# Closing a second scatter table at expert 50 and adding its rows between the last experts of a mixture-of-experts layer

## The chip, the cores and the metric

The kernel runs on one core of a Trainium2 chip. The metric is the device time of one execution in microseconds (us). A core has five engines that run side by side, each through its own queue of instructions: TensorE (PE in the profile; PEld is its weight load), VectorE (DVE), ScalarE (ACT), GpSimd (POOL) and SyncE (SP). SP, ACT and POOL also issue DMA transfers; all of them are carried by the same 16 DMA engines of the core.

## The reference, cut to what matters

The program is a stack of two gated blocks on 2048 tokens of width 512: a token-routed cross-attention layer, a quantized feed-forward layer, a real attention layer and, last, a mixture of experts. The change lies in the mixture of experts alone:

```python
E, K, H, F = (64, 6, 512, 192)
# each token picks K=6 of 64 experts; an expert takes at most CAP=96 slots here
h = silu(einsum('ech,ehf->ecf', buf, w_gate)) * einsum('ech,ehf->ecf', buf, w_up)
out = einsum('ecf,efh->ech', h, w_down)
y = segment_sum(gathered * w, tok, num_segments=Tn)      # each row back to its token
shared = silu(x @ ws_gate) * (x @ ws_up) @ ws_down       # one expert that sees all tokens
return (y + shared)
x = x + tanh(g_ffn[1]) * (y + shared)
```

So the output of a token is its residual row, plus six weighted expert rows, plus the shared expert's row.

## The kernel before, in words

Three stages come first (two layers up to about 520 us, then attention and routing up to about 920 us). Routing leaves in DRAM the normalized rows with their expert weights (`h_rows`), and in SBUF the table `idx`, which says for each expert which token sits in each of its 96 slots. The residual rows have been stored in `out` already (line 897). The shared expert's hidden values of all 16 row tiles lie in SBUF (`shared_a`, 128 rows by 192, for each tile), its down weights too (`shared_dn`).

The expert stage is a loop over 64 experts (line 1195), written as a software pipeline. Iteration `e` issues, in this order of the program:

- `gather(e + 6)`: POOL fetches the 96 rows of a later expert by an indirect DMA (line 1129) into one of six `xg` buffers.
- `turn(e + 2)`: four TensorE transposes of the gathered rows (line 1142), and a DVE copy to `gT` (line 1144).
- `turn_hidden(e)`: two transposes of the hidden values (line 1165), and a DVE copy to `eaT` (line 1167).
- `hidden(e + 1)`: gate and up product in one PSUM tile `gu_ps` (line 1152), Silu on ACT (line 1154), the product with the routing weight on DVE (line 1156).
- `finish(e)`: the down product `e_y` (line 1175), a copy to one of four `e_o` buffers on ACT (line 1177), and an indirect DMA on POOL that adds the 96 rows into a table in DRAM (line 1178). Then the weights of expert `e + 15` are loaded into the buffers that expert `e` leaves (`load_expert`, lines 756, 757 and 759, all issued by SP).

The adding DMAs are kept from overlapping on one table, so the kernel has two tables: even experts add into `out`, odd ones into `more_rows`, which was filled with zeros at the start (line 315). From expert 61 on (`LAST = 3`) all add into `out`. After iteration 61 the program allocates six `rest` tiles in the `e_gu` buffers of experts that are done and loads the 16 row tiles of `more_rows` into them (line 1211, SP). After the loop, for each of the 16 tiles: two transposes of the shared hidden values (`turn_shared`, lines 1217 and 1219), the shared down product `sh_y` (line 1227), one DVE instruction that scales it and adds it to the tile of `rest` (line 1229), and a plain POOL DMA that adds the tile into its 128 rows of `out` (line 1230).

PSUM tiles come from two pools: three buffers for the transposes (`ps_t`) and five for the products (`ps_m`); the shared expert uses the same ones. Weights sit in two pools, `ew` with eight buffers and `ew2` with seven, so 15 experts are loaded ahead. This loop isn't under `manual_schedule`, unlike the stages before it: the framework's planner sets each engine's order from the program order and its own costs, and adds the waits. On DRAM tensors it goes by the regions that an access names: a scatter names the whole table, `out[:, :]`, a plain add 128 rows of it.

Of the kernel before, what the change touches and what calls it, by code (L numbers as in the profile page):

```python
# [9 lines left out]
F32 = mybir.dt.float32  # L10
# [4 lines left out]
ALU = mybir.AluOpType  # L15
# [4 lines left out]
P = 128  # L20
B, S, D = 4, 512, 512
T = B * S
NT = T // P
# [13 lines left out]
E, TOPK, F, GRP = 64, 6, 192, 8  # L37
FH = F // 2
# [8 lines left out]
def flamingo_kernel(  # L47
# [21 lines left out]
    nc = tc.nc  # L69
# [12 lines left out]
    more_rows = dram.tile([TP, D], F32, name="more_rows")  # L82
# [17 lines left out]
    ident = keep.tile([P, P], F32, name="ident")  # L100
# [14 lines left out]
    def after(ins, others):  # L115

        for other in others:
            tc.add_manual_dep(
                ins.ins, other.ins.name, mybir.DependencyInfo(mybir.DependencyClass.Sync, mybir.DependencyReason.DATA),
                reason="what the table holds",  # L120
            )
# [63 lines left out]
    with (  # L185
# [114 lines left out]
        with tc.tile_pool(name="route0", bufs=1) as rp:  # L300
# [54 lines left out]
            while step < NT:  # L355
                a, o = scan[cur], scan[1 - cur]
# [72 lines left out]
        tg_at, half_f1, w_gain, tg_f0_256 = (factors[:, i : i + 1] for i in range(4))  # L429
# [320 lines left out]
    ew = ctx.enter_context(tc.tile_pool(name="ew", bufs=8, side="right"))  # L750
    loaded = {}

    def load_expert(e, ew):

        gu = ew.tile([P, 2, KC, F], F32, name="e_gu", tag="e_gu")
        nc.sync.dma_start(gu[:, 0, :, :], e_gate[e].rearrange("(p k) f -> p k f", k=KC))
        nc.sync.dma_start(gu[:, 1, :, :], e_up[e].rearrange("(p k) f -> p k f", k=KC))
        dn = ew.tile([FH, 2, D], F32, name="e_dn")
        nc.sync.dma_start(dn, e_down[e].rearrange("(p c) d -> p c d", c=2))
        loaded[e] = gu, dn, ew  # L760
# [3 lines left out]
    shared_a = moe.tile([P, NT, F], F32, name="shared_a")  # L764
    shared_dn = moe.tile([FH, 2, D], F32, name="shared_dn")
# [7 lines left out]
    with (  # L773
# [284 lines left out]
        for n in range((NT + 5) * KC):  # L1058
            j, i = divmod(n, KC)
# [39 lines left out]
            else:  # L1099
# [7 lines left out]
                if j == NT:  # L1107
                    at_pool.__exit__(None, None, None)
                    context_pool.__exit__(None, None, None)
                    ew2 = ctx.enter_context(tc.tile_pool(name="ew2", bufs=7))  # L1110
# [3 lines left out]
    with (  # L1114
        tc.tile_pool(name="ex", bufs=2) as xp,
        tc.tile_pool(name="ps_g", bufs=3, space=PSUM) as ps_t,
        tc.tile_pool(name="ps_e", bufs=5, space=PSUM) as ps_m,
    ):

        idx = xp.tile([CAP, E], I32, name="idx", bufs=1)  # L1120
        after(nc.scalar.dma_start(idx, taken[1 : CAP * E + 1, :].rearrange("(s e) o -> s (e o)", e=E)), taken_by)


        tables = out, more_rows
        LAST = 3
        gathered = {}
        def gather(e):
            g = xp.tile([CAP, D + E], F32, name="xg", bufs=6)
            nc.gpsimd.indirect_dma_start(  # L1129
                out=g[:, :],  # L1130
                out_offset=None,
                in_=h_rows[:, :],
                in_offset=bass.IndirectOffsetOnAxis(ap=idx[:, e : e + 1], axis=0),
            )
            gathered[e] = g

        def turn(e):

            g = gathered.pop(e)
            ps = ps_t.tile([P, KC, CAP], F32, name="g_ps", tag="t")  # L1140
            for k in range(KC):
                nc.tensor.transpose(ps[:, k, :], g[:, bass.ts(k, P)], ident[:CAP, :CAP])  # L1142
            gT = xp.tile([P, KC, CAP], F32, name="gT", bufs=3)
            nc.vector.tensor_copy(gT, ps)  # L1144
            return g, gT

        def hidden(e, g, gT):

            gu = loaded[e][0]
            ps = ps_m.tile([CAP, 2, F], F32, name="gu_ps", tag="m")  # L1150
            for k in range(KC):
                nc.tensor.matmul(ps, gT[:, k, :], gu[:, :, k, :], start=k == 0, stop=k == KC - 1)  # L1152
            s = xp.tile([CAP, F], F32, name="s")
            nc.scalar.activation(s, ps[:, 0, :], AF.Silu)  # L1154
            a = xp.tile([CAP, F], F32, name="a")
            nc.vector.scalar_tensor_tensor(  # L1156
                a.rearrange("q (c p) -> q p c", c=2), s.rearrange("q (p c) -> q p c", c=2),
                g[:, D + e : D + e + 1], ps[:, 1, :].rearrange("q (p c) -> q p c", c=2), ALU.mult, ALU.mult,
            )
            return a  # L1160

        def turn_hidden(a):
            ps = ps_t.tile([FH, 2, CAP], F32, name="ea_ps", tag="t")
            for c in range(2):
                nc.tensor.transpose(ps[:, c, :], a[:, bass.ts(c, FH)], ident[:CAP, :CAP])
            aT = xp.tile([FH, 2, CAP], F32, name="eaT")
            nc.vector.tensor_copy(aT, ps)
            return aT

        def finish(e, aT):  # L1170

            _, dn, held = loaded.pop(e)
            y = ps_m.tile([CAP, D], F32, name="e_y", tag="m")
            for c in range(2):
                nc.tensor.matmul(y, aT[:, c, :], dn[:, c, :], start=c == 0, stop=c == 1)  # L1175
            o = xp.tile([CAP, D], F32, name="e_o", bufs=4)
            nc.scalar.copy(o, y)  # L1177
            nc.gpsimd.indirect_dma_start(  # L1178
                out=tables[e % 2 if e < E - LAST else 0][:, :],
                out_offset=bass.IndirectOffsetOnAxis(ap=idx[:, e : e + 1], axis=0),  # L1180
                in_=o[:, :],
                in_offset=None,
                compute_op=ALU.add,
            )
            later = e + ew.bufs + ew2.bufs
            if later < E:
                load_expert(later, held)


        AHEAD = 6  # L1190
        for e in range(AHEAD):
            gather(e)
        turned = {0: turn(0), 1: turn(1)}
        acts = {0: hidden(0, *turned.pop(0))}
        for e in range(E):
            if e + AHEAD < E:
                gather(e + AHEAD)
            if e + 2 < E:
                turned[e + 2] = turn(e + 2)
            aT = turn_hidden(acts.pop(e))  # L1200
            if e + 1 < E:
                acts[e + 1] = hidden(e + 1, *turned.pop(e + 1))
            finish(e, aT)
            if e == E - LAST:


                rest = []
                for held in (ew, ew, ew, ew, ew2, ew2):
                    rest.append(held.tile([P, 3, D], F32, name="rest", tag="e_gu"))
                for j in range(NT):  # L1210
                    nc.sync.dma_start(rest[j // 3][:, j % 3, :], more_rows[bass.ts(j, P), :])


        def turn_shared(j):
            ps = ps_t.tile([FH, 2, P], F32, name="a_ps", tag="t")
            for c in range(2):
                nc.tensor.transpose(ps[:, c, :], shared_a[:, j, bass.ts(c, FH)], ident)
            aT = xp.tile([FH, 2, P], F32, name="aT")
            nc.scalar.copy(aT, ps)
            return aT  # L1220

        aT = turn_shared(0)
        for j in range(NT):
            y = ps_m.tile([P, D], F32, name="sh_y", tag="m")
            this, aT = aT, turn_shared(j + 1) if j + 1 < NT else None
            for c in range(2):
                nc.tensor.matmul(y, this[:, c, :], shared_dn[:, c, :], start=c == 0, stop=c == 1)
            o = rest[j // 3][:, j % 3, :]
            nc.vector.scalar_tensor_tensor(o, y, half_f1, o, ALU.mult, ALU.add)
            nc.gpsimd.dma_start(out[bass.ts(j, P), :], o, accum_op=ALU.add)  # L1230


# [27 lines left out]
```

## Time and profile before

| what | value |
|---|---|
| median of three runs | 1287.63 us (1286.29 to 1292.52) |
| the profiled execution, its own time | 1289.68 us |
| its span in the profile | 1287.9 us |
| TensorE busy | 1036.6 us (80% of the span) |
| VectorE busy | 797.3 us (62%) |
| ScalarE busy | 568.6 us (44%) |
| GpSimd busy | 385.4 us (30%) |
| DMA, by SP's queue | 128.04 MB, 33.2% of 16 engines' span |
| DMA, by POOL's queue | 45.16 MB, 18.0% of 16 engines' span |
| scatters of expert rows, issue to landing | 3.9 / 9.2 / 10.5 us (least, median, most) |
| loads of `rest`, issue to landing | median 6.2 us |
| adds of `rest` into `out`, issue to landing | median 9.7 us |

The span runs from the first to the last instruction of the program on the core; the time of the execution is 1.8 us longer. Shares of busy time are averages over stages with quite different limits, so what the change is worth has to be read from the expert stage, and there from its last 120 us. A transfer's time "to landing" runs from the start of the instruction that issues it to the moment when its semaphore says that all data are there.

### The profile page before, as it was taken

To read this page: it belongs to the slowest core of one execution; us is meant where nothing else is said; L and a number is where in the kernel's file an instruction comes from. 1 tells how busy PE (TensorE), PEld (TensorE's weight loads), DVE (VectorE), ACT (ScalarE), POOL (GpSimd) and SP (SyncE) were. 2 spreads that over 40 slices of the span, in tenths; PEclk is the share of its full clock that TensorE was granted. 3 is DMA by queue.
4 is the path that set the end of the run, shared out by engine and by line. 5 is a ranking of instruction groups with operands and counts; after the bars stand their busy time and mean duration, and the time that the engine had idled before them with its cause. 6 is when DMAs were issued, how large, how long until landed. Compare 5 with 4: busy or idle time off the path is not lost.

```text
span 1287.9 us, 14860 instructions
## 1 busy us (share of the span) xinstructions
PE 1036.6 (80%) x4603; PEld 526.6 (41%) x4603; DVE 797.3 (62%) x1981; ACT 568.6 (44%) x1128; POOL 385.4 (30%) x538
## 2 busy tenths in 40 slices
PE   4498999358888887679888888883499999999994
PEld 3244444123433333344444444441255555544441
DVE  7799999769999997547667676664122222222221
ACT  3766665366767564455555555540011111111120
POOL 3023222100000000012343434346244444444434
PEclk9698999769999999688999999996699999999997
DMA  9844343311111111961111110007699999999978
GB/s 331 293 105 108 91 98 81 83 33 33 33 17 17 21 22 20 279 192 43 60 43 60 43 52 27 36 28 196 179 295 271 279 263 269 271 275 272 265 207 137
DMA packets 75805, 174.75 MB, mean 136 GB/s; under 512 B 13024, under 2 KB 14064, under 8 KB 75664
## 3 DMA queue, kind: packets, MB, share of 16 engines
q1 hardware_dynamic: 51696, 128.04, 33.2%
q0 software_dynamic: 23200, 45.16, 18.0%
q8 instruction: 37, 0.61, 0.2%
q10 hardware_dynamic: 832, 0.62, 0.2%
q14 instruction: 40, 0.33, 0.1%
HBM read 133.76 MB, written 44.20 MB: 138 GB/s over the span
## 4 chain that ended last, share of the span: by engine, by line
DVE 34%; PE 32%; DMA 19%; ACT 7%; issue 5%; POOL 2%; SPq 0%; DVEq 0%; POOLq 0%; ACTq 0%
DMA out_dram<-e_o,idx 13%; PE gu_ps L1152 5%; PE at_s L833 4%; PE at_o L884 4%; PE l_mm L473 3%; DVE mx_top L586 3%; DVE low L838 3%; PE e_y L1175 3%; PE p_ps L857 3%; DVE inter L655 3%; PE first_ps L934 3%; DVE mx_q L602 3%; DVE w_q L265 2%; DVE w_src L262 2%; ACT p L847 2%
## 5 line engine op out<-in xcount | busy, mean ns | idle before, releaser
L1152 PE MATMUL gu_ps<-e_gu,gT 128*96 128x384 f32 x512 | 179.6, 494 | 0.2 <-DVE gT L1144 0.2
L838 DVE TENSOR_REDUCE low<-at_s 128x2 f32<-128x1024 f32 x64 | 78.2, 1222 | 92.3 <-PE at_s L833 92.3
L1156 DVE SCALAR_TENSOR_TENSOR a<-s,xg,gu_ps 96x192 f32<-96x192 f32 x64 | 35.0, 548 | 152.1 <-ACT s L1154 152.1
L847 ACT ACTIVATE p<-at_s,low 128x512 f32<-128x512 f32 x128 | 86.7, 683 | 91.0 <-DVE low L838 91.0
L1175 PE MATMUL e_y<-e_dn,eaT 96*96 96x512 f32 x256 | 120.5, 593 | 0.1
L125 POOL DMA_INDIRECT taken<-token_no,to_i x96 | 96.4, 1004 | 48.0 <-issue 24.7
L1152 PEld LDWEIGHTS gu_ps<-e_gu,gT 128*96 128x96 f32 x512 | 79.7, 166 | 63.6 <-issue 63.6
L857 PE MATMUL p_ps<-ident,p 128*128 128x128 f32 x512 | 81.8, 299 | 26.4 <-DVE place L1022 13.0
L1144 DVE COPY gT<-g_ps 128x384 f32<-128x384 f32 x64 | 35.7, 557 | 100.6 <-PE g_ps L1142 73.7
L1177 ACT COPY e_o<-e_y 96x512 f32<-96x512 f32 x64 | 37.2, 581 | 137.1 <-DMA out_dram<-e_o,idx 56.2
L857 PEld LDWEIGHTS p_ps<-ident,p 128*128 128x128 f32 x512 | 61.1, 151 | 82.6 <-ACT pT L858 29.9
L833 PE MATMUL at_s<-c_tile,q 64*128 64x512 f32 x256 | 80.4, 709 | 13.5 <-DMA first_w<-in_L_ffn_gate_w_dram 13.5
L667 POOL DMA_DIRECT2D x_rows<-y_sb x16 | 13.6, 853 | 258.7 <-ACT y_sb L666 258.7
L858 ACT COPY pT<-p_ps 128x512 f32<-128x512 f32 x128 | 70.0, 590 | 38.2 <-PE p_ps L857 38.1
L1178 POOL DMA_INDIRECT out_dram<-e_o,idx x34 | 48.8, 1434 | 118.8 <-ACT e_o L1177 65.6
L490 POOL DMA_INDIRECT x_rows<-y_sb,to_row x19 | 39.0, 2053 | 149.9 <-ACT y_sb L489 149.9
L1129 POOL DMA_INDIRECT xg<-h_rows,idx x64 | 59.7, 933 | 65.2 <-DVE a L1156 31.4
L641 PEld LDWEIGHTS <-hT 128*128 128x128 bf16 x512 | 50.0, 101 | 70.1 <-issue 13.1
L473 PE MATMUL l_mm<-cT,sT 128*128 x152 | 76.4, 650 | 0.0
L641 PE MATMUL gu<-wgT,hT 128*128 128x512 bf16 x256 | 70.8, 402 | 6.4 <-ACT hT L622 6.4
L473 PE MATMUL l_mm<-cT,hT 128*128 x152 | 71.1, 612 | 1.7 <-ACT hT L460 1.7
L1154 ACT ACTIVATE s<-gu_ps 96x192 f32<-96x192 f32 x64 | 20.9, 326 | 116.8 <-PE gu_ps L1152 116.7
(226 smaller groups left out, 2025.1 us busy)
## 6 DMA issues: line engine op xcount, KB each, us to landing
e_gu<-in_L_ffn_w_gate_dram SPq DMA_DIRECT2D x64, 384.0 KB, 16.1
e_gu<-in_L_ffn_w_up_dram SPq DMA_DIRECT2D x64, 384.0 KB, 16.1
e_dn<-in_L_ffn_w_down_dram SPq DMA_DIRECT2D x64, 384.0 KB, 15.9
w_src<-in_L_ffn_w_gate_dram SPq DMA_DIRECT2D x8, 512.0 KB, 5.4
c_sb<-in_ctx_dram SPq DMA_DIRECT2D x4, 1024.0 KB, 8.3
w_src<-in_L_ffn_w_up_dram SPq DMA_DIRECT2D x8, 512.0 KB, 4.8
more_rows<-zeros SPq DMA_DIRECT2D x16, 256.0 KB, 8.1
w_src<-in_L_ffn_w_down_dram SPq DMA_DIRECT2D x8, 512.0 KB, 4.5
```

Source lines behind the costliest of these rows:

```text
L125: ins = nc.gpsimd.indirect_dma_start(out=table[:, :], out_offset=bass.IndirectOffsetOnAxis(ap=to, axis=0), in_=what, in_offset=None)
L473: nc.tensor.matmul(ps.unsqueeze(1), aT[:, k, :], cT[:, bass.ds(at + k, 1), :], start=k == 0, stop=k == KC - 1)
L641: nc.tensor.matmul(ps, hT[:, k, :], wT[:, k, bass.ts(c, 512)], start=k == 0, stop=k == KC - 1)
L833: nc.tensor.matmul(s[:, h, :], t["q"][rows, bass.ts(i, P)], t["c"][rows, :], start=True, stop=True)
L838: nc.vector.tensor_reduce(low, tiles[j]["s", i], AX.X, ALU.max, negate=True)
L847: nc.scalar.activation(p[:, h, :], s[:, h, :], AF.Exp, bias=low[:, h : h + 1], accum_out=t["sums"][:, i, h : h + 1])
L857: nc.tensor.transpose(ps[:, k, :], p[:, h, bass.ts(k, P)], ident)
L858: nc.scalar.copy(tiles[j]["pT"][h][:, :, bass.ts(i, P)], ps)
L884: nc.tensor.matmul(o[bass.ts(h, HD), :], cT[:, j // 4 * KC + k, bass.ds((j % 4) * P + h * HD, HD)], pT[h][:, k, :], start=k == 0, stop=k = ...
L1129: nc.gpsimd.indirect_dma_start(out=g[:, :], out_offset=None, in_=h_rows[:, :], in_offset=bass.IndirectOffsetOnAxis(ap=idx[:, e : e + 1], a ...
L1152: nc.tensor.matmul(ps, gT[:, k, :], gu[:, :, k, :], start=k == 0, stop=k == KC - 1)
L1175: nc.tensor.matmul(y, aT[:, c, :], dn[:, c, :], start=c == 0, stop=c == 1)
```

## The change

Three things are changed, all in the expert stage. First, `more_rows` is closed earlier: experts up to 49 alternate between the two tables as before, and experts 50 to 63 all add into `out` (before: 61 to 63). Second, the six `rest` tiles are allocated and loaded in iterations 51 (two of them), 52, 53, 54 and 55, ahead of that iteration's `finish`. Third, the work on the shared expert is no longer a loop of its own at the end. In iterations 51 to 61 one or two of its tiles are transposed, and the product and combination of the tile before are done; then, after `finish` of experts 53, 55, 57, 59 and 61, the three tiles of one `rest` buffer are added into `out`, and after `finish` of 62 the sixteenth tile. The number of instructions and bytes stays as it was, and each `rest` tile is added to `out` by the same kind of DMA.

```diff
-        LAST = 3
+        CLOSED = 50
...
-                out=tables[e % 2 if e < E - LAST else 0][:, :],
+                out=tables[e % 2 if e < CLOSED else 0][:, :],
...
+        def other_rows(c):
+            held = ew if c < 4 else ew2
+            rows = held.tile([P, 3, D], F32, name="rest", tag="e_gu")
+            for j in range(3 * c, min(3 * c + 3, NT)):
+                nc.sync.dma_start(rows[:, j % 3, :], more_rows[bass.ts(j, P), :])
+            rest.append(rows)
+
+        def turn_shared(j):
...
+
+        def shared_out(j, aT):
+            y = ps_m.tile([P, D], F32, name="sh_y", tag="m")
+            for c in range(2):
+                nc.tensor.matmul(y, aT[:, c, :], shared_dn[:, c, :], start=c == 0, stop=c == 1)
+            o = rest[j // 3][:, j % 3, :]
+            nc.vector.scalar_tensor_tensor(o, y, half_f1, o, ALU.mult, ALU.add)
+
+        def add_rest(c):
+            for j in range(3 * c, min(3 * c + 3, NT)):
+                nc.gpsimd.dma_start(out[bass.ts(j, P), :], rest[c][:, j % 3, :], accum_op=ALU.add)
+
+        rest, shared, turned_a = [], deque(range(NT)), deque()
...
             if e + 1 < E:
                 acts[e + 1] = hidden(e + 1, *turned.pop(e + 1))
+            late = e - CLOSED
+            if late == 1:
+                other_rows(0)
+            if 1 <= late <= 5:
+                other_rows(late)
+            for _ in range(2 - late % 2 if 1 <= late < 12 else 0):
+                if shared:
+                    j = shared.popleft()
+                    turned_a.append((j, turn_shared(j)))
+                    if len(turned_a) > 1:
+                        shared_out(*turned_a.popleft())
             finish(e, aT)
-            if e == E - LAST:
...
+            if late >= 3 and late % 2 == 1 and late < 12:
+                while turned_a and turned_a[0][0] < 3 * ((late - 3) // 2 + 1):
+                    shared_out(*turned_a.popleft())
+                add_rest((late - 3) // 2)
+            if late == 12:
+                while turned_a:
+                    shared_out(*turned_a.popleft())
+                add_rest(5)
```

`turn_shared` is the function of before. The old loop over 16 tiles after the experts, with its loads of `rest` after iteration 61, is taken out.

More of the change, by code (lines that the diff above doesn't have):

```diff
@@ L1187, in finish @@
                 load_expert(later, held)
+        def other_rows(c):
[5 more added lines that the diff above has]
+        def turn_shared(j):
+            ps = ps_t.tile([FH, 2, P], F32, name="a_ps", tag="t")
+            for c in range(2):
+                nc.tensor.transpose(ps[:, c, :], shared_a[:, j, bass.ts(c, FH)], ident)
+            aT = xp.tile([FH, 2, P], F32, name="aT")
+            nc.scalar.copy(aT, ps)
+            return aT
+        def shared_out(j, aT):
+            y = ps_m.tile([P, D], F32, name="sh_y", tag="m")
+            for c in range(2):
+                nc.tensor.matmul(y, aT[:, c, :], shared_dn[:, c, :], start=c == 0, stop=c == 1)
[5 more added lines that the diff above has]
+        rest, shared, turned_a = [], deque(range(NT)), deque()
         AHEAD = 6
@@ L1202, in flamingo_kernel @@
                 acts[e + 1] = hidden(e + 1, *turned.pop(e + 1))
-            finish(e, aT)
-            if e == E - LAST:
[L1207 to L1230, printed above, removed]
+            late = e - CLOSED
[9 more added lines that the diff above has]
+                        shared_out(*turned_a.popleft())
+            finish(e, aT)
+            if late >= 3 and late % 2 == 1 and late < 12:
[6 more added lines that the diff above has]
+                add_rest(5)
 _INS = ['x', 'itok_BxS_13_99985', 'ctx_2048', 'g_xattn', 'g_ffn', 'L0_ffn_w_gate', 'L0_ffn_w_up', 'L0_ffn_w_down',
```

## The prediction, made before the changed kernel was seen

> **What bounds the kernel now.** I read the chain of work that ended last, then the DMA views of its last 120 us, then the queues of GpSimd (POOL) and SyncE (SP). The page puts 13% of the span on one line of the chain, the scatter of expert rows into the output. In order of time around expert 50:
>
> ```profile
> 1168.97 9.65 DMA out_dram<-e_o,idx
> ...
> 1179.42 9.46 DMA out_dram<-e_o,idx
> ...
> 1189.68 9.48 DMA out_dram<-e_o,idx
> ...
> 1199.96 9.80 DMA out_dram<-e_o,idx
> ```
>
> One scatter-add into `out` starts 0.7 to 0.8 us after the one before it has landed, so they form a serial chain, about 10.3 us a link. Experts alternate between `out` and `more_rows`, so there are two such chains side by side, and one link pays for two experts: 5.1 us an expert, hardly above TensorE's 4.8 us (the spacing of the gu_ps pieces early in the stage, 932.22, 937.02, 941.81). Counting back from the last scatter (expert 63, at 1254.29), the one at 1189.68 is expert 50's.
>
> A link takes 9.5 us because the DMA engines are full. The stretches 1190 to 1215 and 1253 to 1260 (PE, PEld, DVE, ACT, POOL busy; then clock, DMA share, GB/s):
>
> ```profile
> 1190.00:1215.00 25.00, 23.23 (x88) 11.75 (x89) 6.67 (x16) 4.34 (x10) 12.87 (x11) 1.00 1.06 263
> ...
> 1253.00:1260.00 7.00, 7.00 (x22) 3.25 (x21) 2.55 (x4) 1.28 (x4) 1.40 (x1) 1.00 0.23 28
> ```
>
> When the loads are over, the same scatter is much shorter. POOL's timeline (start, duration, idle time before) shows starts 4.7 and 5.05 us apart (1230.46 to 1235.14 to 1240.19), and the DMA view gives 3.9 us to landing for the scatter at 1230.46:
>
> ```profile
> 1230.46 1.40 POOL L1178 DMA_INDIRECT out_dram<-e_o,idx  x1 [4.54 <-ACT e_o L1177]
> ...
> 1235.14 1.40 POOL L1178 DMA_INDIRECT out_dram<-e_o,idx  x1 [1.45 <-DMA out_dram<-e_o,idx]
> 1240.19 1.40 POOL L1178 DMA_INDIRECT out_dram<-e_o,idx  x1 [3.65 <-ACT e_o L1177]
> 1248.18 1.40 POOL L1178 DMA_INDIRECT out_dram<-e_o,idx  x1 [6.59 <-DMA out_dram<-e_o,idx]
> 1254.29 1.40 POOL L1178 DMA_INDIRECT out_dram<-e_o,idx  x1 [4.71 <-issue]
> 1260.05 3.59 POOL L1230 DMA_DIRECT2D out_dram<-rest  x4 [4.35 <-DVE rest L1229]
> ```
>
> The last view is SP's queue:
>
> ```profile
> 1211.82 0.33 SPq L756 DMA_DIRECT2D e_gu<-in_L_ffn_w_gate_dram  x1
> 1214.00 0.33 SPq L757 DMA_DIRECT2D e_gu<-in_L_ffn_w_up_dram  x1
> 1215.71 2.26 SPq L759 DMA_DIRECT2D e_dn<-in_L_ffn_w_down_dram  x2
> 1236.46 3.81 SPq L1211 DMA_DIRECT2D rest<-more_rows  x8
> ```
>
> The load of expert 63's weights belongs to iteration 48, whose down product ran near 1164 (expert 51's ran at 1178.4, less three times 4.8), but SP issues it at 1211.8 to 1217.6: **SP is some 50 us behind the program**, held by its own DMAs (about eight in flight, 15 to 17 us each), and they land until 1232.
>
> [...] no scatter into `out` starts before its forerunner has landed, and the first add of the tail (1260.05) starts after the last scatter landed (1258.35). [...] 9.5 us to landing beside the loads, 3.9 us without. [...]
>
> **The change, part by part.**
>
> *The second table closes at 50.* Scatters of experts 50 to 63 all go to `out`. Before, nine of them did (50, 52, 54, 56, 58, 60 to 63). The program order makes `out` a chain of 14 scatters with six add groups A0 to A5 among them, in this order: 50 51 52 53 A0 54 55 A1 56 57 A2 58 59 A3 60 61 A4 62 A5 63. A group's adds touch only a few rows, but each scatter names the whole table, so it waits for the group, and the group for the scatter before it. That is 20 links.
>
> *Prices.* A lone scatter link: 4.07 us to landing (mean of 3.91, 4.29, 4.06, all with no loads) plus 0.76 from landing to the next start = 4.83. A loaded one: 9.9 (slightly under 10.3, since only one scatter is in flight; bounds 8.8+0.8, the scatter at 1220.84, and 10.3). A group of three: the tail's first three adds were issued at 1260.05, 1260.66 and 1261.23 and landed at 1263.96, 1266.13 and 1267.42, so 7.4 us; the first starts 1.7 us after the scatter lands (1258.35 to 1260.05): 9.1. A group of one: 1.7 + 3.9 = 5.6.
>
> *The loads of `rest`.* They move from iteration 61 to 51 to 55, but on SP they stay behind the loads of experts up to 63. From 1190 on the changed kernel has fewer scatters and gathers in flight: about five scatters of 0.197 MB and four gathers of 0.221 MB fewer by 1232, 1.9 MB, at 265 GB/s 7 us. So the weights end near 1225 instead of 1232, the first tiles of `rest` land at about 1226, 1227 and 1228, and the last near 1237 (before, tiles followed each other by 0.67 us).
>
> *The shared expert's work.* 16 times (transposes 0.22, matmuls 1.72, copy 0.37 on ACT, 0.75 on DVE): 1.94 us a tile on TensorE, 31 us. It moves among the experts. Beside links of 5 to 10 us it hides: a pair of experts has 18.8 us per period below and needs 2x4.8 + 3x1.94 = 15.4. If that cover were gone it would cost up to 31 us; it isn't on the path.
>
> *The new wait on DVE.* The combination of tile 0 is traced in iteration 52 and waits for `rest`. Iteration 52 ran at about 1180 to 1185 on TensorE. Behind the waiting instruction in DVE's queue stand gT of expert 55 and eaT of expert 53, so expert 53's down product waits until about 1228. This happens if the planner, which orders this loop, takes `rest` for early. SP's queue says that it does: the gate and up loads of 63 stand ahead of a down load of 62 (two down loads follow each other at 1215.71), an order in which loads are issued as slots come free, with no backlog. So I take the stall; its bounds are zero and the case below.
>
> *The sum.* 50 at 1189.7, 51 at 1199.6, 52 at 1209.5, landed 1218.7. DVE free at about 1228; eaT 0.3, e_y 1.9, copy 0.6 and hand-overs bring 53 to 1231.5. Beside `rest` it lands after 6.7 us (6.25 us between the 7.23 and 5.35 of the two scatters that did so before, with some weight traffic on top): 1238.2. A0 lands 9.1 later: 1247.3. Then four periods of two scatters and a group (2x4.83 + 9.1 = 18.8): 1322.3. Scatter 62: 1327.1. A5: 1332.7. Scatter 63: 1337.6. From the last landing to the end of the span were 3.6 us (1284.3 to 1287.9): **span 1341**, 53.3 us more than 1287.9. What goes is the tail of 16 adds (28 us from 1260); it is in the sum, since the span's end is rebuilt from expert 50 on. The profiled execution's own time, 1289.68, becomes 1343; the median of 1287.63, 2.05 less, becomes 1341.
>
> **Rivals.**
> *No DVE stall* (the planner puts the combinations later): 53 starts at 1219.4 and lands near 1228, but A0 still needs the third tile, so it starts at about 1232, lands (beside loads) at 1240.5, and the rest of the sum gives a span of 1334, a median of 1334. For it: the planner does reorder (each gather stands one scatter early). Chance 0.22.
> *Dearer links*: gathers and late `rest` loads stay beside the scatters, 5.3 us a lone link and 10 a group: ten times 0.5 and five times 0.9 more, 1350. For it: 7.23 us at 1240. Chance 0.13.
> *Scatters don't wait for the groups*: six group links fall out of 1341, 51 us (5x9.1 + 5.6): 1290, no change. Against it: the adds did wait for the scatter. Chance 0.03.
> *Faster*: the wait for `out` is no bound, and TensorE is. From expert 52's down product at 1183.2, eleven experts of 4.8 and 31 us of shared work bring expert 63's to 1267; product, copy, scatter and end (1.9 + 1 + 4.1 + 3.6) give 1277. It decides only if the 20 links average under 4.7 us (1284.3 less 1189.7, over 20). The shortest lone scatter link in the trace is 4.7 and a group is 9.1. Chance 0.04.
>
> **How the numbers follow.** Forecast 0.58, the others 0.22, 0.13, 0.03, 0.04. The range takes in the unstalled case with loaded links at 9.6 and a cheaper group (8.3: 7.4 plus 0.9, the step that POOL itself shows), 1334 less 9, and the dear case, 1350, plus 3: 1325 to 1353. Some 0.5% is what a measurement of this kernel can tell from no change; faster 0.04, same 0.03, slower 0.93.
>
> **What will show it.** Right: scatters 50 to 63 in one chain with the groups among them; the last link a scatter with no tail of adds after it; `rest` loads on SP no earlier than about 1210; a DVE wait of some 40 us on `rest`; DMA nearly idle after 1240. Wrong: `rest` loads among the weights before 1200, scatters that start before a group landed, or lone links far from 4.8.

## The result, and the profile after

The changed kernel takes 1337.24 us (median of four runs, 1332.39 to 1348.18), the kernel before 1288.57 us in the same comparison (1286.29 to 1292.52). The ratio is 1.0386 with a 95% interval of 1.0313 to 1.0459: slower, by some 49 us. The profiled execution took 1348.18 us, with a span of 1346.3 us; it is the slowest of the four, so its sums end some 11 us above the median.

Up to expert 50 nothing has moved: its scatter starts at 1190.55 us (before: 1189.68). All that is lost is lost after it. From that scatter to the end of the span were 98.2 us before; now they are 155.7.

First GpSimd's timeline after the change (start, duration, then in brackets the idle time before it and what ended it):

```profile
1190.55 1.45 POOL L1178 DMA_INDIRECT out_dram<-e_o,idx  x1 [4.52 <-DMA out_dram<-e_o,idx]
...
1200.44 1.44 POOL L1178 DMA_INDIRECT out_dram<-e_o,idx  x1 [7.20 <-DMA out_dram<-e_o,idx]
...
1210.88 1.45 POOL L1178 DMA_INDIRECT out_dram<-e_o,idx  x1 [7.75 <-DMA out_dram<-e_o,idx]
...
1239.32 1.44 POOL L1178 DMA_INDIRECT out_dram<-e_o,idx  x1 [3.01 <-ACT e_o L1177]
1244.81 2.77 POOL L1215 DMA_DIRECT2D out_dram<-rest  x3 [4.05 <-DMA out_dram<-e_o,idx]
...
1253.54 1.48 POOL L1178 DMA_INDIRECT out_dram<-e_o,idx  x1 [4.64 <-DMA out_dram<-rest]
...
1258.62 1.44 POOL L1178 DMA_INDIRECT out_dram<-e_o,idx  x1 [2.34 <-ACT aT L1203]
1263.16 2.78 POOL L1215 DMA_DIRECT2D out_dram<-rest  x3 [3.10 <-DMA out_dram<-e_o,idx]
```

Every start into `out` now waits for the one before it. The three scatters 50, 51 and 52 are 10 us apart, while the weights still load (DMA share 1.05 from 1190 to 1215, 260 GB/s). Then there is a hole of 28.4 us between 52 and 53. From 1244.81 on a group of three adds takes 8.5 to 9.1 us up to the next scatter, and a lone scatter 4.5 to 5.1, once 6.2.

The hole comes from VectorE, whose timeline has one long wait, and TensorE stands behind it. Below are the lines of the two engines, each from its own timeline:

```profile
1184.87 0.55 DVE L1156 SCALAR_TENSOR_TENSOR a<-s,xg,gu_ps 96x192 f32<-96x192 f32 x1 [2.29 <-ACT s L1154]
1232.50 1.41 DVE L1211 SCALAR_TENSOR_TENSOR rest<-sh_y,factors,rest 128x512 f32<-128x512 f32 x2 [47.09 <-DMA rest<-more_rows]
```

```profile
1193.19 1.88 PE L1209 MATMUL sh_y<-shared_dn,aT 96*128 96x512 f32 x4
1234.69 3.73 PE L1175 MATMUL e_y<-e_dn,eaT 96*96 96x512 f32 x4 [39.62 <-DVE eaT L1167]
...
1245.91 1.88 PE L1175 MATMUL e_y<-e_dn,eaT 96*96 96x512 f32 x4
```

And the reason for that wait stands in SyncE's queue. The loads of `rest`, traced in iteration 51, are issued behind the last weights:

```profile
1213.68 0.33 SPq L756 DMA_DIRECT2D e_gu<-in_L_ffn_w_gate_dram  x1
1215.42 0.33 SPq L757 DMA_DIRECT2D e_gu<-in_L_ffn_w_up_dram  x1
1217.02 1.94 SPq L759 DMA_DIRECT2D e_dn<-in_L_ffn_w_down_dram  x2
1220.44 16.84 SPq L1195 DMA_DIRECT2D rest<-more_rows  x16
```

The stretches of the tail (PE, PEld, DVE, ACT, POOL busy; granted clock, DMA share, GB/s) show what no longer limits:

```profile
1215.00:1232.00 17.00, 0.00 (x0) 0.00 (x0) 0.00 (x0) 0.00 (x0) 0.00 (x0) 0.50 1.01 247
...
1242.00:1300.00 58.00, 58.00 (x202) 28.52 (x201) 19.12 (x34) 10.68 (x27) 20.03 (x18) 1.00 0.50 76
1300.00:1343.00 43.00, 9.04 (x26) 3.67 (x24) 1.91 (x4) 2.07 (x4) 12.32 (x11) 0.67 0.46 62
```

From 1215 to 1232 no engine computes at all. From 1242 to 1300 TensorE is busy without a gap, catching up, while the DMA engines are half idle. After 1300 TensorE is nearly done, and 43 us remain in which little happens but one DMA after another.

**A trap in the chain view.** The chain of work that ended last goes through TensorE between 1234 and 1301, and enters the DMAs only here:

```profile
1300.93 0.37 DVE eaT L1167
1301.30 0.11 issue
1301.41 1.15 POOL out_dram L1215 x2
1302.56 6.55 DMA out_dram<-rest
```

Read literally, the group at 1301.41 waited for a copy of expert 62's hidden values, which it doesn't use. The copy merely ended 0.1 us earlier. The scatter of expert 59, started at 1296.69, landed at 1300.88, and that is what the group had to wait for. TensorE's timeline says the same: from expert 54 on it is always ahead. The down product of 55 begins at 1252.64 and that of 61 at 1298.85, and they take 1.9 us; their scatters start at 1258.62 and 1314.91. Whether `out` or TensorE sets the pace is then put to the test.

### The profile page after: what moved, and what is told of

Its sections match the earlier page's. It is cut to its first block, busy times and chain, and to the rows that moved or that the text cites. A ratio compares the mean times of both kernels' runs of the same rounds, so it can differ in the third digit from the quotient of the medians.

```text
span 1346.3 us, 14852 instructions
## 1 busy us (share of the span) xinstructions
PE 1035.4 (77%) x4603; PEld 525.3 (39%) x4603; DVE 797.3 (59%) x1981; ACT 568.8 (42%) x1128; POOL 388.8 (29%) x538
## 4 chain that ended last, share of the span: by engine, by line
PE 37%; DVE 32%; DMA 19%; ACT 6%; issue 4%; POOL 1%; SPq 0%; DVEq 0%; POOLq 0%; ACTq 0%
PE gu_ps L1152 9%; PE e_y L1175 6%; DMA out_dram<-e_o,idx 4%; PE at_s L833 3%; PE l_mm L473 3%; DVE mx_top L586 3%; PE at_o L884 3%; DMA e_gu<-in_L_ffn_w_up_dram 3%; DVE low L838 3%; DVE inter L655 3%; DVE mx_q L602 2%; PE first_ps L934 2%; DMA e_dn<-in_L_ffn_w_down_dram 2%; PE p_ps L857 2%; DVE w_q L265 2%
## 5 line engine op out<-in xcount | busy, mean ns | idle before, releaser
L1178 POOL DMA_INDIRECT out_dram<-e_o,idx x39 | 56.8, 1456 | 145.7 <-DMA out_dram<-e_o,idx 53.2
L833 PE MATMUL at_s<-c_tile,q 64*128 64x512 f32 x256 | 80.4, 710 | 14.6 <-DMA first_w<-in_L_ffn_ws_gate_dram 14.6
L667 POOL DMA_DIRECT2D x_rows<-y_sb x16 | 13.8, 861 | 258.6 <-ACT y_sb L666 258.6
L1175 PEld LDWEIGHTS e_y<-e_dn,eaT 96*96 96x96 f32 x256 | 41.8, 165 | 97.7 <-issue 55.6
```

The costliest lines, as they stand in the source:

```text
L833: nc.tensor.matmul(s[:, h, :], t["q"][rows, bass.ts(i, P)], t["c"][rows, :], start=True, stop=True)
L1178: nc.gpsimd.indirect_dma_start(out=tables[e % 2 if e < CLOSED else 0][:, :], out_offset=bass.IndirectOffsetOnAxis(ap=idx[:, e : e + 1], ax ...
```

## The experiments

The theory: the 14 scatters and six groups form one serial chain on `out`, and that chain sets the end. The wait of VectorE costs only what it delays a scatter. The main rival: the loss is the 47 us wait of VectorE with TensorE idle behind it, and the late scatters merely follow. A second rival: TensorE's work, now with the shared expert in it, is the bound. In this section "tail" is the time from the start of expert 50's scatter to the end of the span, in the profiled execution of each kernel.

**One part alone: the table closes at 50, all else as before.**

```diff
-        LAST = 3
+        LAST = 14
```

> The kernel before with one part of the change alone: the second table closes at expert 50 (LAST = 14), the loads of rest follow iteration 50, and the shared expert and its 16 adds stay after the experts, so VectorE waits for nothing new. Theory: 14 scatters in one chain, 9.9 us each until the weights have landed and 4.8 after that, end near 1281, then 16 adds: a median near 1309. Rival (the wait of VectorE is the loss): about 1288, as before.

Measured: 1309.83 us (1305.59 to 1310.10), ratio 1.0164 (1.0133 to 1.0195), tail 122.8 us. VectorE has no wait on `rest` here and the shared expert's work hasn't moved (only the loads of `rest` start earlier, with the closing of the table), yet 22 us of the 49 are there. GpSimd's timeline, where loaded links give way to unloaded ones:

```profile
1213.99 1.44 POOL L1178 DMA_INDIRECT out_dram<-e_o,idx  x1 [7.10 <-ACT e_o L1177]
...
1223.84 1.44 POOL L1178 DMA_INDIRECT out_dram<-e_o,idx  x1 [7.17 <-ACT e_o L1177]
...
1239.23 1.44 POOL L1178 DMA_INDIRECT out_dram<-e_o,idx  x1 [4.97 <-ACT e_o L1177]
1244.14 1.43 POOL L1178 DMA_INDIRECT out_dram<-e_o,idx  x1 [3.47 <-ACT e_o L1177]
1249.06 1.40 POOL L1178 DMA_INDIRECT out_dram<-e_o,idx  x1 [3.49 <-ACT e_o L1177]
...
1273.76 1.40 POOL L1178 DMA_INDIRECT out_dram<-e_o,idx  x1 [3.47 <-ACT aT L1219]
1279.59 10.66 POOL L1230 DMA_DIRECT2D out_dram<-rest  x12 [4.42 <-DVE rest L1229]
```

Nearly 10 us a link while the weights load, 7.7 us for two links beside the last loads (not shown), 4.9 us after. The rival has no place for this loss: the chain makes it. The tail grew by 24.6 us for five experts (51, 53, 55, 57 and 59) that moved from one table to the other.

**The wait of VectorE shortened: loads of `rest` on GpSimd's queue.**

```diff
-                nc.sync.dma_start(rows[:, j % 3, :], more_rows[bass.ts(j, P), :])
+                nc.gpsimd.dma_start(rows[:, j % 3, :], more_rows[bass.ts(j, P), :])
```

> The changed kernel with one edit: the loads of rest are issued by GpSimd instead of SyncE, so that they no longer stand behind the weight loads; the order on TensorE, VectorE and ScalarE stays the same. Theory (the serial chain on out sets the end; the wait of VectorE costs only what it delays scatter 53): the wait on rest shrinks from 47 us to some 20, A0 lands about 8 us earlier, and the median goes from 1337 to about 1329. Rival (the wait of VectorE, and TensorE idle behind it, is the loss): the median falls by the 25 us that the wait shrinks, to about 1312.

Measured: 1341.48 us (1339.09 to 1345.86), ratio 1.042 (1.0384 to 1.0457). The wait did shrink, to 19.05 us before the first combination and 2.1 before the second:

```profile
1202.85 0.75 DVE L1211 SCALAR_TENSOR_TENSOR rest<-sh_y,factors,rest 128x512 f32<-128x512 f32 x1 [19.05 <-DMA e_dn<-in_L_ffn_w_down_dram]
```

The view names a weight load as what ended the first wait. The instruction reads no weights, though, and `sh_y` was long done (1.88 us from 1182.03), so it must have been the landing of the first tile of `rest` about then; the second wait is put down to `rest`. Nothing came back, where the rival said 1312. It misses the theory's 1329 too, and GpSimd's timeline says why:

```profile
1193.52 0.62 POOL L1195 DMA_DIRECT2D rest<-more_rows  x1 [8.99 <-DMA e_gu<-in_L_ffn_w_gate_dram]
...
1196.33 1.52 POOL L1178 DMA_INDIRECT out_dram<-e_o,idx  x1 [0.30 <-DMA e_gu<-in_L_ffn_w_up_dram]
...
1208.14 1.54 POOL L1178 DMA_INDIRECT out_dram<-e_o,idx  x1 [2.97 <-DMA out_dram<-e_o,idx]
...
1223.57 1.53 POOL L1178 DMA_INDIRECT out_dram<-e_o,idx  x1 [1.50 <-DMA rest<-more_rows]
```

The first load waits for the last scatter into `more_rows`, started at 1183.10, and scatter 50 stands behind it. The view puts these 8.99 us down to a weight load; in the run with both edits below it names the scatter, for a wait of 8.2 us. Then the loads stand between the scatters: 50 to 51 takes 11.8 us, 51 to 52 15.4, 52 to 53 13.9. The first group starts at 1242.0, hardly before the 1244.8 of the changed kernel. The edit took the pause out of the chain and put it back as longer links. Since it changed both at once, this run alone doesn't decide between theory and rival.

**The chain halved: odd experts from 51 on add elsewhere.** Their rows are left out of the output.

```diff
-        tables = out, more_rows
+        tables = out, more_rows, third
...
-                out=tables[e % 2 if e < CLOSED else 0][:, :],
+                out=tables[e % 2 if e < CLOSED else 2 * (e % 2)][:, :],
```

> The changed kernel, but odd experts from 51 on add into a third table that nobody reads; their rows are left out of the output. The chain on out loses 7 of its 14 scatters, the wait of VectorE on rest stays. Theory: the end is then set by TensorE, whose queue ended near 1308 in the profile, plus the last links: about 1319 in the profile's time, a median near 1310. Rival (the wait of VectorE is the loss): no change, about 1337.

Measured: 1312.92 us (1311.45 to 1326.47), ratio 1.0233 (1.0172 to 1.0293), tail 123.3 us. VectorE still waits 38.7 us on `rest` in one piece, and 24 us of the median come back. So the wait can't be the whole loss: it is nearly as long as in the change, and half of the loss is gone. Now TensorE is the bound, as its timeline shows: two experts and three shared tiles every 15.4 us, back to back. It starts late, behind the wait, so with the chain halved the wait may count for more: the tail is still 25 us longer than in the kernel before. How much of that is the wait was not measured.

```profile
1220.25 1.41 DVE L1212 SCALAR_TENSOR_TENSOR rest<-sh_y,factors,rest 128x512 f32<-128x512 f32 x2 [38.71 <-DMA rest<-more_rows]
```

```profile
1248.92 1.88 PE L1176 MATMUL e_y<-e_dn,eaT 96*96 96x512 f32 x4
...
1264.32 1.88 PE L1176 MATMUL e_y<-e_dn,eaT 96*96 96x512 f32 x4
...
1279.72 1.88 PE L1176 MATMUL e_y<-e_dn,eaT 96*96 96x512 f32 x4
```

**Both edits together** (odd experts' rows from 51 on left out).

> Both edits together: loads of rest issued by GpSimd, and odd experts from 51 on add into a third table (their rows are left out). Theory: with the chain halved and the wait shrunk to 20 us TensorE is the bound from expert 53 on: about 1290. Rival: the wait alone counts, as with the loads on GpSimd: about 1312.

Measured: 1313.33 us (1304.12 to 1317.25), ratio 1.0209 (1.018 to 1.0238), tail 117.1 us. The number is the rival's, the mechanism isn't. The longest wait of VectorE on `rest` is 11.8 us, and TensorE's last down product starts at 1269.3, 33 us before the end of a span of 1302.2. What ends last is the chain again.

```profile
1190.49 0.75 DVE L1212 SCALAR_TENSOR_TENSOR rest<-sh_y,factors,rest 128x512 f32<-128x512 f32 x1 [11.79 <-DMA rest<-more_rows]
```

```profile
1269.29 1.96 PE L1176 MATMUL e_y<-e_dn,eaT 96*96 96x512 f32 x4 [0.94 <-DVE eaT L1168]
```

The loads on GpSimd's queue hold scatter 52 back to 1211.24, 26 us after 50. From then on the groups start 13.7 us apart (1237.8 to 1278.9 in three steps), about one lone link and one group. The theory's 1290 was missed: it had forgotten that the loads would delay the chain, and the run with the loads on GpSimd alone shows the same fault.

**The same adds in fewer groups** (these lines stand in place of the two `if late` blocks that add the groups).

```diff
+            done = {5: (0, 1), 9: (2, 3), 12: (4, 5)}.get(late, ())
+            while done and turned_a and turned_a[0][0] < 3 * (done[-1] + 1):
+                shared_out(*turned_a.popleft())
+            for c in done:
+                add_rest(c)
```

> The changed kernel with the same 16 adds in three groups instead of six: six tiles after expert 55, six after 59, four after 62. Theory (each group is a link of the chain on out and pays a start and a landing latency, whatever its size): two groups of three cost 18.2 us with their hand-overs, one of six about 13 (a sixth add of a burst lands 11.4 us after the first is issued in the tail of the kernel before); so 5 us less twice and 4 less for the last, a median near 1323. Rival (the bytes of the adds, or TensorE, set the pace): no change, about 1337.

Measured: 1329.89 us (1328.81 to 1336.03), ratio 1.0356 (1.0307 to 1.0405). By the medians it is 7 us faster than the change, and the intervals overlap. The tail is 141.1 us against 155.7, that is 14.6 less, where 14 were forecast; but these are two single executions, and that of the change was the slowest of its four. The links themselves bear it out. A group of six takes 12.1 to 13.9 us up to the next scatter, where two groups of three took 17.4 and 17.6 in the change, and the last four tiles take 10.3 instead of 13.8; together 12.7 us of the 14.6.

```profile
1248.46 5.36 POOL L1215 DMA_DIRECT2D out_dram<-rest  x6 [3.05 <-DMA out_dram<-e_o,idx]
...
1262.31 1.47 POOL L1178 DMA_INDIRECT out_dram<-e_o,idx  x1 [7.18 <-ACT aT L1203]
...
1282.83 5.32 POOL L1215 DMA_DIRECT2D out_dram<-rest  x6 [3.38 <-DMA out_dram<-e_o,idx]
1294.90 1.51 POOL L1178 DMA_INDIRECT out_dram<-e_o,idx  x1 [6.74 <-ACT e_o L1177]
```

The bytes are the same, and three groups fewer save some 4.2 us each (12.7/3). That is about a hand-over and the landing of a first add: an estimate from the change's own profile, where the one took 0.3 to 0.55 us and the other 3.9 to 4.2.

**The groups later, so that VectorE meets `rest` when it is nearly there.**

```diff
-            for _ in range(2 - late % 2 if 1 <= late < 12 else 0):
+            for _ in range(2 if 6 <= late else 0):
...
+            done = {8: (0,), 9: (1,), 11: (2,), 12: (3,), 13: (4, 5)}.get(late, ())
```

> The changed kernel with the shared expert's work and the groups moved later: two tiles in each of iterations 56 to 63, groups of three after experts 58, 59, 61 and 62, and the last four tiles after 63. VectorE meets rest when it has nearly landed, so scatters 53 to 57 follow 52 without the pause of 19 us. Theory: the chain has the same 14 scatters and 16 adds; only the pause goes (about 11 us, since the links that take its place are still loaded) and one group is merged (4 us): about 1331 in the profile's time, a median near 1322. Rival (the wait of VectorE is the loss): 30 us or more come back, about 1305 or less.

Measured: 1329.77 us (1323.59 to 1335.01), ratio 1.0323 (1.0267 to 1.038). The median is 7.5 us under the change's, and the intervals overlap again. The tail is 138.5 us, 17.2 less than 155.7 (theory: 15). The 30 us of the rival aren't there, though the wait on `rest` went from 47.1 us to 15.07:

```profile
1231.52 0.75 DVE L1211 SCALAR_TENSOR_TENSOR rest<-sh_y,factors,rest 128x512 f32<-128x512 f32 x1 [15.07 <-DMA rest<-more_rows]
```

Scatters 52 to 55 follow each other without a hole (1215.77, 1226.34, 1234.78, 1242.56). Link by link, the adds (five groups instead of six, the last without a scatter behind it) take 5.6 us less than in the change. So the pause of VectorE is worth some 12 us of the tail in this kernel, not 30.

**The other way round: the table closes later than before.**

```diff
-        LAST = 3
+        LAST = 1
```

> The other way round: the kernel before with the second table closed later (LAST = 1, only expert 63, and 62 by its parity, add into out at the end; the loads of rest follow expert 63's iteration). Theory: the chain on out at the end is shorter by the scatter of 61 and the loads of rest collide with fewer scatters, so the last scatter lands near 1250 instead of 1258 and the end comes 6 to 9 us earlier: a median near 1281. Rival: the loads of rest, which start some 5 us later, move onto the path and take the place of the chain: no change, 1286 to 1290.

Measured: 1280.33 us (1275.66 to 1283.18), against 1287.76 for the kernel before beside it: ratio 0.9953 (0.9929 to 0.9977), tail 94.0 us. The scatters of the last experts come in turn, and the adds start 64.8 us after expert 50's scatter instead of 70.4:

```profile
1234.80 1.40 POOL L1178 DMA_INDIRECT more_rows<-e_o,idx  x1 [0.66 <-ACT aT L1219]
1237.61 1.40 POOL L1178 DMA_INDIRECT out_dram<-e_o,idx  x1 [1.40 <-DMA out_dram<-e_o,idx]
1242.59 1.40 POOL L1178 DMA_INDIRECT out_dram<-e_o,idx  x1 [3.58 <-ACT aT L1219]
1251.79 9.77 POOL L1230 DMA_DIRECT2D out_dram<-rest  x11 [7.79 <-issue]
```

By its interval this version is some 0.5% faster than the kernel before, and so beats both kernels, by little.

**Never closed** (LAST = 0, `rest` loaded after iteration 63).

> The kernel before with the two tables alternating to the end (LAST = 0; expert 63 adds into the second table; the loads of rest follow iteration 63). Theory: no single chain is left, out is done near 1245; the loads of rest start near 1243 and share the DMA engines with the adds: loads 10.7 us and adds 20.5 us after 1243, then the last landing and the end: 1278 to 1281. Rival: the adds wait for the loads and the end stays at 1286 to 1290 or later.

Measured: 1283.82 us (1277.14 to 1294.22), ratio 0.9977 (0.9956 to 0.9998), tail 93.5 us. The adds begin at 1244.96, the earliest of all. That is 58.9 us after expert 50's scatter, 5.9 us sooner than with LAST = 1, yet the tail is only 0.5 us shorter; where the rest goes is not shown. The median lies between the theory's 1281 and the rival's 1286, so the run doesn't decide between the two. By its interval it is hardly faster than the kernel before.

## Why the prediction was right

It said 1341 us in a range of 1325 to 1353, by a chain of 20 links and a pause of VectorE; the median is 1337.24. The mechanism is the one that it named: one chain on `out`, and a pause of VectorE that delays the chain. The number is nearer than its terms deserve, since errors of both signs are in the sum. The steps one by one:

- **The chain on `out` as the bound:** shown. Closing the table costs 22 us with only the loads of `rest` moved beside it; halving the chain gives 24 us back with VectorE's wait still there; fewer groups and a shorter pause cut the tail by about the forecast amounts. From the links, an estimate of where the 57.5 us between the two tails come from: some 25 from the closed table, 10 to 12 from the pause, and some 23 because the 16 adds go in six groups between scatters instead of in one.
- **Loaded links, 9.9 us:** measured 9.9 and 10.4.
- **Lone links, 4.83 us:** too low by a little. From one scatter to the next it measured 5.0 to 5.1, once 6.2, and 4.5 to 4.8 where a group follows, since the hand-over, from a landing to the next start, is shorter there (4.9 again and again in the run that only closes the table). Landing takes 4.0 to 4.3 us.
- **A group of three, 9.1 us:** right only in sum. The hand-over of 1.7 us, read from the first add of the old tail, was too long: it measured 0.3 to 0.55. The landing was underrated: 7.7 to 8.3 us, not 7.4. From scatter landing to group landing that is 8.4. The dearer lone links make up for it: one period of two scatters and a group was forecast at 18.8 us; from the first group to the fifth it measured 74.94/4 = 18.7.
- **`rest` behind the weights on SyncE:** shown. Its size was off. The weights landed at 1231.8, not 1225. They did load faster, as it had said (1.84 us for each load from 1190 on, before 2.11), but 16 of them were still to be issued at that time, not 14 as before. So the first tile landed at 1232.2, where 1226 had been said.
- **VectorE stalls on `rest` in iteration 52:** shown, for 47 us. So the planner did place the combination early, as the prediction read from the order of SyncE's loads; that this is how the planner reckons was not tested.
- **Scatter 53 at 1231.5:** it started at 1239.3. Some 6 us come from the late tile. The rest comes from the down product, 3.73 us instead of 1.88 (last section).
- **The price of the pause, 7 us** (the stalled case, 1341, less the unstalled, 1334): too small. The run with later groups puts it at some 12.
- **The shared expert's work is hidden:** shown, with little to spare. TensorE needed 15.4 of 18.7 us for two experts and three tiles, and after the pause it was ahead of the scatters again by expert 54. One link, from 56 at 1271.86 to 57 at 1278.02, took 6.2 us though TensorE was ahead; its cause stays open (1.2 us). With the chain halved TensorE became the bound, as the rival on the faster side had it, but with a span of 1309.6, not 1277: behind the pause it started late.
- **The sum from scatter 50 to the end:** 151.5 us forecast, 155.7 measured. The late scatter 53 puts in 7.0. Its landing (5.2 us instead of 6.7) and the first group (8.1 from landing to landing instead of 9.1) take out 2.5, and what follows differs by 0.2. The two errors have different causes, so that they cancel in part is luck.
- **The range:** the terms named for its lower end, 9 us below 1334, give only about 6 (three loaded links of 0.3, five groups of 0.8 and the group of one).

Of the signs named in advance these came as said: a last link that is a scatter with no tail of adds, and `rest` issued from 1220.44 on. The DMA engines, forecast as nearly idle after 1240, were half busy (share 0.50 and 0.46), though they moved only 62 to 76 GB/s.

The median itself can't settle the last few us: the executions of the changed kernel spread over 16 us. The start of scatter 50 alone differs by nearly 10 us between profiles of kernels that are the same up to there (1185.1 to 1194.7). What sets it wasn't looked into. That is why the tails were compared, and each tail is from a single execution.

## What to carry to other kernels

Before work is moved "into the gaps" of a loop, count what it will wait for, not what it computes. In the changed kernel every scatter into `out` and every group of adds started only after the one before it had landed, so each was a link of one serial chain: 4.9 us or more from one lone scatter of 197 KB to the next, 4.0 to 4.3 us of it from issue to landing. Two tables gave two chains side by side, and each expert that was moved from the second to the first added about a full link (24.6 us for five), so the second table should close late; closing it for expert 63 alone was the best of the versions measured, half a percent below the kernel before. An early place in the program isn't an early place in time: the loads of `rest`, traced in iteration 51, stood behind all the weight loads that SyncE's queue had still to issue and went out from 1220.44 us on. VectorE's next instruction needed them, so that backlog became a pause of 47.09 us.

## What the runs showed of the hardware that was not expected

TensorE came back from its wait at half speed. The down product of expert 53, the first after 39.62 us of idleness, took 3.73 us, against 1.88 for the next one (at 1245.91), and the granted clock was 0.50 in the idle stretch from 1215 to 1232, 0.61 in the ten us after it and 1.00 from 1242 to 1300. In the run with both edits the first down product after 6.78 us of idleness took 3.73 us as well, and the next one 1.88.

The same adds cost less in one burst. In the old tail the adds of 256 KB land 1.28 us apart once they flow, while in the change the first of a group takes 3.9 to 4.2 us to land. One group of 16 cost 24 us in the old tail and the same 16 in six groups 47 (five of 8.4 and one of about 4.5).
